# Four attention layers on one core: a copy, additions, gathers, first queries and grouped projections at other places in a hand-written order

## The chip, the cores and the metric

The kernel runs on one core of a Trainium2 chip, on inputs in fp32. The core has TensorE for matmuls (PE in the profile; its weight loads are PEld), VectorE (DVE), ScalarE (ACT), GpSimd (POOL) and SyncE (SP), which issues most DMAs. Matmuls write PSUM, eight banks of 2 KB for each of 128 partitions; TensorE, VectorE and ScalarE use it. The metric is the time of one execution on the device in microseconds (us), as a median over runs.

## The reference

Four residual layers of cross-attention follow each other on `x` of shape (4, 512, 256); the context is (4, 1024, 512). Layers 0, 2 and 3 are alike, "masked", with 16 heads of 64; layer 1 is "grouped", with 16 query heads of 16 that share 4 key and value heads.

```python
# layers 0, 2 and 3 (hidden_states 512 x 256, encoder_hidden_states 1024 x 512, of each of 4 batches)
q, k, v = hidden_states @ Wq, encoder_hidden_states @ Wk, encoder_hidden_states @ Wv
...
logits = jnp.einsum('bhqd,bhkd->bhqk', q, k) * scale + col_bias
out = jnp.einsum('bhqk,bhkd->bhqd', softmax(logits), v)
return out @ Wo + bo + residual
# layer 1
xn = rmsnorm(x, norm_w)
q, k, v = xn @ wq, cond @ wk, cond @ wv
...
attn = softmax(jnp.einsum('bgrtd,bsgd->bgrts', qg, k) * scale)
return residual + jnp.einsum('bgrts,bsgd->btgrd', attn, v) @ wo
```

`col_bias` adds -20 times one minus a mask to the columns of four tokens.

## The kernel before

**Units and steps.** The work is cut into units: one layer, one batch, two masked heads, or a half of a group of grouped heads (`u` from 0 to 7; `h` is `u % 2`). Ninety-six masked and thirty-two grouped units are laid out by `MASKED_TURNS` and `GROUPED_TURNS` into 96 steps, one masked unit `g` each, and in the steps 12 to 19, 22 to 29, 32 to 39 and 68 to 75 a grouped unit `lam` beside it. There is no scheduler: the order in which the last loop calls the helpers is the order of the instructions on each engine.

**A masked unit.** In its step `scores` makes eight tiles of 128 keys by two heads by 512 queries (L854, for the first tile also L860 with the mask), ScalarE copies each to SBUF (L864), and VectorE finds a maximum over them (L871 or L911, then `max_quarters` and `max_everywhere`, L927 to L951). VectorE subtracts it (L959), ScalarE takes exponentials (L965), and POOL sums them (L1004, 7 a unit). In the next step the unit is `g1`: `attend` multiplies with the values (L887), and its sums are turned into reciprocals either on VectorE alone (`normalise`, L911 and L1036 to L1047, then L1073) or with a matmul by ones (`sums_beside`, L1059 and L790 to L792, then L1073). The step after projects two such units together (`project_out`, L1091) and VectorE adds the result to the state (L1113).

**A grouped unit.** In the step before its own it is `coming`: `logits_pair` makes two tiles of logits at a time (L827), which ScalarE copies (L833) and VectorE reduces (`block_max`, L911); there are four such pairs. In its own step POOL subtracts the maximum (L957, 8 a unit), ScalarE takes exponentials, and `attend_grouped` multiplies with the values (L887, 128x32). ScalarE copies one half of the product to SBUF (`keep_even`, L897), VectorE adds the other (`keep_odd`, L901), and after two units (`h` is 1) `turn_grouped` normalises it (L1014 to L1020) and sends it to DRAM or gets the other part from there (L1022, L1025). After four units the grouped projection follows (L1091 and L1113).

**Keys, values, queries.** Keys and values of a pair of masked units are made from the transposed context (`keys`: L540 with the copy L545; `values`: L588, L595). In steps where the third set of buffers is free they are made with seven products in place of eight (`fast_keys`, `fast_values`, L648): POOL first combines weights (L631, four) and, for a batch that is new (`fresh`), the context (L620, four). In `seven_products` the copy L671 of the sixth product into another's bank must be there before that bank and the sixth product's own go on. `project_q` (L751, copy L756) makes the queries of the next masked unit, `follows`. For a first unit of a later layer it stands last but one in the step.

**Loading.** A batch's context rows are gathered by indirect DMAs from POOL (`part_ctx`, L395, each 128 rows), transposed on TensorE at the end of the step (L408, called `rests` in the loop) and kept in DRAM. Steps 1 to 8 do it for batches 1 to 3, two gathers a step up to step 4 and four from step 5.

**The order inside a step.** `fill` is a list of pieces with estimated costs. The loop calls them in turn; `events` (subtractions and exponentials) are let in by estimated time, and `pairs` of a coming grouped unit likewise. A piece's function issues its matmuls and may return a function that issues what follows them on other engines. `late` holds work that runs in `behind_exponentials`, which comes before the first pair of logits, or at the end of the step. `by_ones` is true where a step has both `lam` and `coming`: 28 of the 32.

**PSUM.** `Place` hands out banks: two together, or one. Where both `lam` and `coming` are there (`tabled`), two together come from banks 0 to 3 (scores also 4 and 5) and single ones from 4 to 7. It takes the bank that has been given back the longest in the order of the program (`back`), so what is called later changes which bank the next one gets, and whose last read it waits for:

```python
at = min((n for n in among if n in free), key=lambda n: free[n])
```

Of the kernel before, what the change touches and what calls it, by code (L numbers as in the profile page):

```python
# [80 lines left out]
def kernel(ctx: ExitStack, tc: tile.TileContext, a: dict, out: bass.AP):  # L81
# [740 lines left out]
    def logits_pair(g, i):  # L822
        ws = [Place(), Place()]
        for odd in range(2):
            for j in range(2):
                rows = slice(64 * odd + 32 * j, 64 * odd + 32 * (j + 1))
                nc.tensor.matmul(  # L827
                    ws[odd].ap[:, j * S : (j + 1) * S], lhsT=g.kt[rows, i * P : (i + 1) * P],
                    rhs=g.qt[rows, :], start=True, stop=True,
                )  # L830
        for odd, w in enumerate(ws):
            t = 2 * i + odd
            nc.scalar.copy(g.st[t], w.ap)  # L833
            if tabled[0]:
                w.back()
                block_max(g, t)
            elif t == 0:
                g.mx_place = w
            else:
                w.back()  # L840
                top = g.mx_place.ap
                nc.vector.tensor_tensor(top, top, g.st[t], ALU.max)
# [56 lines left out]
    def keep_odd(g):  # L899
        half = gq[g.b, "o"][64 * g.h : 64 * (g.h + 1), :]  # L900
        nc.vector.tensor_tensor(half, half, g.po[64:128, :], ALU.add)  # L901
        if g.h == 0:
            g.place.back()
# [172 lines left out]
    def project_out(*of):  # L1076

        g = of[0]
        x, acc = xs[g.l, g.b], xs.get((g.l + 1, g.b))
        opens = acc is None  # L1080
        if opens and g.masked:
            acc = new_state(g.l + 1, g.b)
        elif opens:

            acc = xs[g.l + 1, g.b] = x
            x_at[g.l + 1, g.b] = x_at[g.l, g.b]
        w = Place()
        m = w.ap
        for k in range(KC):
            for each in of:  # L1090
                nc.tensor.matmul(  # L1091
                    m[:, k * S : (k + 1) * S], lhsT=each.wo[:, k * P : (k + 1) * P], rhs=each.ot,
                    start=each is g, stop=each is of[-1],
                )
        y = m.rearrange("p (k q) -> p k q", q=S)

        def add_last(q):
            nc.vector.tensor_tensor(acc[:, :, q], y[:, :, q], acc[:, :, q], ALU.add)

        def add():  # L1100
            if g is masked[-1]:
                for i in range(0, NI, 2):
                    add_last(slice(i * P, (i + 2) * P))
                    store(g.b, range(i, i + 2))
                left[g.b] = -1
            elif opens and g.masked:
                bo = columns[f"L{g.l}_xattn_bo"]
                for k in range(KC):
                    nc.vector.scalar_tensor_tensor(
                        acc[:, k, :], y[:, k, :], bo[:, k : k + 1], x[:, k, :], ALU.add, ALU.add  # L1110
                    )
            else:
                nc.vector.tensor_tensor(acc, y, x if opens else acc, ALU.add)  # L1113
            w.back()

        left[g.b] -= len(of)
        return add
# [50 lines left out]
    parts = {}  # L1168
# [19 lines left out]
    rests = [p() for p in parts[-1]]  # L1188
    g0, g1 = masked[0:2]
# [23 lines left out]
    def values(of):  # L1213
        if of.masked:
            return [(1.8, lambda n=n, h=h: v_pair(of, n, h)) for n in range(NI) for h in range(2)]
        return [(1.4, lambda n=n: v_quarter(of, n)) for n in range(4)]

    def idle_set(n):
        if n < 10:
            return 0 < n  # L1220
        return n < len(steps) - 2 and not (
            at(n)[1] or at(n + 1)[1] or at(n + 2)[1] and at(n + 2)[1].first
        )
# [9 lines left out]
    for n in range(len(steps) + 2):  # L1233
# [4 lines left out]
        g1, attended = attended, g  # L1238
        ending = n >= len(steps) - 2

        rests = [p() for p in parts.get(n, ())] if n >= 0 else []
        kk = []
        if g:
            kk = masked[1:2] if n == 0 else masked[g.n + 1 : g.n + 3] if g.n % 2 else []
# [31 lines left out]
        if fast_k or fast_v:  # L1276
            assert 2 in sets_free, n
            combine_weights(kk[0].w["k2"] if fast_k else g.w["v2"])
            fresh = combined_of != (kk[0] if fast_k else g).b
            if fresh:  # L1280
                combined_of = (kk[0] if fast_k else g).b
                combine_context(combined_of)
        else:
            combined_of = None
        if soon and soon.first:
            fetch_whole(soon.b)

# [9 lines left out]
        ready = []  # L1297
        events = []
        late = []
        pairs = []  # L1300

        def pass_events(us):
# [8 lines left out]
        def pair(i):  # L1311
            if i == 0:
                behind_exponentials()
                take_set(coming)
            logits_pair(coming, i)
            if i == NT // 2 - 1:
                max_quarters(coming)
                max_everywhere(coming)
# [44 lines left out]
        if coming:  # L1363
# [3 lines left out]

        fill, of_grouped = (  # L1370
            [
                (1.8 * len(each), lambda each=each: project_out(*each))
                for each in outs if each[0].masked == m
            ]
            for m in (True, False)
        )
        outs = []
        of_queries = []
        if follows and not (follows.l and follows.u == 0):
            of_queries.append((1.7, lambda: project_q(follows)))  # L1380
        if coming and coming.first:
            of_queries += [(1.7, lambda i=i: grouped_q(coming, i)) for i in range(2)]
        if fast_k:
            of_keys = fast_keys(*kk)
            if fresh:
                of_keys[1:4] = of_keys[3:4] + of_keys[1:3]
            fill = of_keys[:2] + fill + of_keys[2:4] + of_queries + of_keys[4:]
        elif fast_v:
            of_values = fast_values(g)
            if fresh:  # L1390
                of_values[1:4] = of_values[3:4] + of_values[1:3]
            fill = of_values[:2] + fill + of_queries + of_values[2:]
        else:
            fill += of_queries
            if kk:
                fill += keys(*kk)
# [3 lines left out]
        if lam:  # L1400

            def attend_grouped():
                while any(of is lam for _, of, _ in events):
                    events.pop(0)[2]()
                lam.v = head(lam).v
                place_out(lam)
                attend(lam)
                give_set(lam)
                late.append(lambda: keep_odd(lam))
                if lam.h == 1:  # L1410
                    late.append(lambda: turn_grouped(lam))
                return lambda: keep_even(lam)

            total, where = 0.0, 0
            while where < len(fill) and total < (8.0 if by_ones and of_values else 9.5):
                total += fill[where][0]
                where += 1
            fill.insert(where, (3.6, attend_grouped))
            if by_ones:
                fill.insert(where, (1.0, lambda: late.insert(0, sums_beside(g1))))  # L1420
        if soon and soon.first:

            def square():
# [8 lines left out]
        if coming and coming.first:  # L1432
            fill += values(coming)
            fill.append((0.0, lambda: drop_whole(coming.b)))
        if follows and follows.l and follows.u == 0:

            fill[-1:-1] = [(1.7, lambda: project_q(follows))]
        if g1 and g and ending:
# [56 lines left out]
```

## Time and profile before

| | |
|---|---|
| median of 3 runs | 3468.09 us (3467.56 to 3470.66) |
| profiled execution | 3467.95 us, span of its instructions 3465.9 |
| mean granted clock of TensorE | 0.999 |
| L1004 on POOL | 668 x 2369 ns |
| L965 on ACT | 1024 x 1058 ns |
| L959 on DVE | 768 x 1212 ns |
| L957 on POOL | 256 x 2381 ns |
| L864 on ACT | 768 x 1047 ns |

The table's lower part is from the profile's list of costliest groups: how often, and how long one is. A group is a line with an engine and a shape; each row also tells how long the engine was idle just before such instructions and what ended most of that. TensorE's matmuls are pipelined, so the duration of one is longer than the distance of two: the distance of two L540 passes on the timeline is 0.43 us, of two L648 of 128 columns 0.11. One fp32 matmul stands there as two passes. The lengths of some steps, from the first scores matmul to the next step's:

| step | us | step | us |
|---|---|---|---|
| 6 | 30.47 | 8 | 32.85 |
| 11 | 49.86 | 31 | 50.17 |
| 12, 22, 68 | 41.54, 41.55, 41.54 | 32 | 42.60 |
| 14, 74 | 40.08, 40.08 | 18, 24, 28, 34, 70 | 40.63, 40.66, 40.63, 40.63, 40.64 |
| 15, 25, 33, 35, 69 | 44.31, 44.31, 44.29, 44.33, 44.33 | 17, 27, 37 | 43.46 each |
| 23, 71 | 44.31, 44.31 | 16, 26, 36, 72 | 41.90, 41.88, 41.91, 41.86 |
| 43, 45 | 31.66, 31.77 | 41, 47, 63, 77 | 34.59, 33.17, 33.18, 37.33 |
| 42, 44 | 28.72, 28.72 | 40, 76 | 32.05, 32.04 |

### The profile page before, as it was taken

How to read it: one execution, taken by the hardware profiler on the slowest of the kernel's cores; microseconds unless marked ns; L12 is line 12 of the kernel's file. 1: busy time of each engine (PE TensorE's matmuls, PEld its weight loads, DVE VectorE, ACT ScalarE, POOL GpSimd, SP SyncE). 2: the span in 40 equal slices, each digit the busy share in tenths (PEclk: the TensorE clock that was granted, in tenths of full speed). 3: DMA queues.
4: the chain of work that ended last, by engine and by line, in shares of the span. 5: the costliest groups of instructions: out<-in, count | busy, mean ns of one | idle time of the engine just before them, and what ended most of it. 6: DMA issues, size and time to landing. Idle time of an engine off the chain costs nothing.

```text
span 3465.9 us, 42986 instructions
## 1 busy us (share of the span) xinstructions
PE 3425.5 (99%) x15634; PEld 1672.4 (48%) x15634; DVE 2970.5 (86%) x3911; ACT 2347.2 (68%) x2727; POOL 2588.8 (75%) x1331
## 2 busy tenths in 40 slices
PE   8999999999999999999999999999999999999998
PEld 4554544445444444444445454554544444454553
DVE  7888788987889878997888888888789987888887
ACT  4676577775877667876566666666677875666664
POOL 5888588884888758888678768677588888769774
PEclk9999999999999999999999999999999999999999
DMA  3232201111100120001001101011101101011100
GB/s 105 64 99 83 78 19 53 34 50 39 54 27 30 46 63 30 26 30 46 27 28 52 40 29 42 28 52 54 39 30 51 36 20 52 28 42 57 30 31 9
DMA packets 146199, 151.71 MB, mean 44 GB/s; under 512 B 23608, under 2 KB 123448, under 8 KB 145476
## 3 DMA queue, kind: packets, MB, share of 16 engines
q1 hardware_dynamic: 142894, 140.05, 12.9%
q0 software_dynamic: 2560, 8.39, 0.8%
q8 instruction: 124, 2.03, 0.2%
q14 instruction: 87, 0.71, 0.1%
q10 hardware_dynamic: 534, 0.52, 0.0%
HBM read 132.15 MB, written 15.73 MB: 43 GB/s over the span
## 4 chain that ended last, share of the span: by engine, by line
PE 90%; DVE 5%; POOL 2%; ACT 2%; issue 1%; DMA 0%; DVEq 0%; ACTq 0%; POOLq 0%
PE ps L887 21%; PE ps L648 18%; PE ps L854 17%; PE ps L588 9%; PE ps L540 8%; PE ps L751 5%; PE ps L827 5%; PE ps L1091 4%; DVE ps L871 1%; POOL st L957 1%; DVE st L959 1%; PE ps L1059 1%; PE ps L728 1%; ACT st L864 1%; PE ps L860 1%
## 5 line engine op out<-in xcount | busy, mean ns | idle before, releaser
L1004 POOL TENSOR_TENSOR st<-st 128x1024 f32<-128x1024 f32 x668 | 1582.5, 2369 | 579.0 <-ACT st L965 534.1
L965 ACT ACTIVATE st<-st 128x1024 f32<-128x1024 f32 x1024 | 1038.9, 1058 | 260.9 <-DVE st L959 136.3
L959 DVE TENSOR_TENSOR st<-st,ps 128x1024 f32<-128x1024 f32 x768 | 883.6, 1212 | 3.3
L887 PE MATMUL ps<-st,v 128*64 128x512 f32 (+1 forms) x4064 | 789.8, 595 | 1.5 <-ACT kt L545 1.5
L957 POOL TENSOR_TENSOR st<-st 128x1024 f32<-128x1024 f32 x256 | 598.1, 2381 | 256.5 <-DVE st L951 256.5
L871 DVE TENSOR_TENSOR ps<-ps,st 128x1024 f32<-128x1024 f32 x476 | 586.7, 1233 | 218.1 <-ACT st L864 174.9
L864 ACT COPY st<-ps 128x1024 f32<-128x1024 f32 x768 | 714.7, 1047 | 79.2 <-PE ps L860 63.9
L854 PE MATMUL ps<-qt,kt 64*128 64x512 f32 x3072 | 712.2, 598 | 6.0 <-DVE every L938 2.6
L911 DVE TRANSPOSE_TENSOR_REDUCE tops<-st 128x32 f32<-128x1024 f32 x448 | 517.1, 1211 | 41.9 <-ACT st L833 41.0
L887 PEld LDWEIGHTS ps<-st,v 128*64 128x64 f32 (+1 forms) x4064 | 239.8, 130 | 536.5 <-issue 447.2
L854 PEld LDWEIGHTS ps<-qt,kt 64*128 64x128 f32 x3072 | 291.5, 186 | 363.4 <-ACT st L864 139.1
L588 PE MATMUL ps<-wv,ctx 128*128 128x256 f32 x1408 | 325.6, 384 | 0.0
L648 PE MATMUL ps<-st 128*128 128x128 f32 (+1 forms) x1572 | 303.3, 341 | 9.9 <-ACT ps L671 7.8
L540 PE MATMUL ps<-ctx,wk 128*128 128x512 f32 x672 | 309.8, 604 | 2.2 <-ACT ctx L420 2.2
L833 ACT COPY st<-ps 128x1024 f32<-128x1024 f32 x256 | 246.7, 1016 | 91.8 <-PE ps L827 91.6
L588 PEld LDWEIGHTS ps<-wv,ctx 128*128 128x128 f32 x1408 | 262.2, 190 | 93.6 <-issue 55.2
L648 PEld LDWEIGHTS ps<-st 128*128 128x128 f32 x1572 | 208.5, 191 | 102.1 <-issue 91.6
L663 ACT COPY st<-ps 128x512 f32<-128x512 f32 x44 | 25.8, 586 | 332.1 <-PE ps L648 332.1
L540 PEld LDWEIGHTS ps<-ctx,wk 128*128 128x128 f32 x672 | 123.4, 191 | 180.0 <-issue 163.4
L751 PE MATMUL ps<-x,wq 128*128 128x512 f32 x384 | 186.3, 608 | 1.3 <-ACT x L383 1.1
L1091 PE MATMUL ps<-ot,wo 128*128 128x512 f32 x384 | 175.2, 598 | 0.7 <-DVE ot L1073 0.7
L827 PE MATMUL ps<-qt,kt 32*128 32x512 f32 x1024 | 171.7, 640 | 1.3 <-ACT st L833 0.7
(190 smaller groups left out, 2980.4 us busy)
## 6 DMA issues: line engine op xcount, KB each, us to landing
ctx<-kept SPq DMA_DIRECT2D x24, 1024.0 KB, 8.1
wk<-in_L_xattn_Wk_dram SPq DMA_DIRECT2D x47, 512.0 KB, 3.6
wv<-in_L_xattn_Wv_dram SPq DMA_DIRECT2D x47, 512.0 KB, 3.6
wq<-in_L_xattn_Wq_dram SPq DMA_DIRECT2D x96, 128.0 KB, 3.6
wo<-in_L_xattn_Wo_dram SPq DMA_DIRECT2D x96, 128.0 KB, 3.7
st<-kept SPq DMA_DIRECT2D x4, 2048.0 KB
qt<-q SPq DMA_DIRECT2D x64, 128.0 KB, 3.7
kept<-st SPq DMA_DIRECT2D x12, 512.0 KB, 3.2
```

What stands on the lines that cost most here:

```text
L540: nc.tensor.matmul(m, lhsT=g.w["k"][:, k, :], rhs=ctx_half[g.b, n][:, k, :], start=(k == 0), stop=(k == KT - 1),)
L588: nc.tensor.matmul(m[:, half * 2 * P : (half + 1) * 2 * P], lhsT=ctx_half[g.b, t // 4][:, k, t % 4 * P : (t % 4 + 1) * P], rhs=g.w["v2"][: ...
L648: nc.tensor.matmul(m if is_keys else m[:, q], lhsT=right[:, k, :] if is_keys else left_[:, k, q], rhs=left_[:, k, :] if is_keys else right ...
L854: nc.tensor.matmul(m[:, j * S : (j + 1) * S], lhsT=g.kt[g.rows[j], keys], rhs=g.qt[g.rows[j], :], start=True, stop=t > 0,)
L864: nc.scalar.copy(g.st[t], m)
L871: nc.vector.tensor_tensor(top, top, g.st[t], ALU.max)
L887: nc.tensor.matmul(g.po[at, :], lhsT=g.v[:, t, rows], rhs=g.st[t][:, j * S : (j + 1) * S], start=(t == first), stop=(t == last),)
L911: nc.vector.tensor_reduce(out_, of.rearrange("p (b x) -> p b x", x=32), AX.X, op, apply_transpose=True)
L957: nc.gpsimd.tensor_tensor(g.st[t], g.st[t], g.mb, ALU.subtract)
L959: nc.vector.tensor_tensor(g.st[t], g.st[t], g.mb, ALU.subtract)
L965: nc.scalar.activation(st, st, AF.Exp)
L1004: nc.gpsimd.tensor_tensor(g.acc, g.st[0] if t == 1 else g.acc, g.st[t], ALU.add)
```

## The change

- In steps that are `by_ones`, `keep_even` (ScalarE's copy of a grouped half) and `keep_odd` with `turn_grouped` no longer run right after the grouped product and in `late`. They go into a new list, `behind_pair`, which is emptied in `pair` right after the next `logits_pair`, thus after the copies of the first pair. In other steps `keep_odd` and `turn_grouped` stay in `late`, as one function.
- In odd steps that are `by_ones`, the addition behind a `project_out` goes into `late` (a new helper, `behind`), thus behind all subtractions of the unit. The turned sums of `sums_beside` are appended to `late` and no longer put at its head.
- `rests`, whose calls issue the gathers and the load of `x`, is made after the combinations of weights and context and not at the head of the step.
- `project_q` for a first unit of a layer stands last but one only where the state it reads is finished late (a new helper, `comes_late`); elsewhere it stands where it does for all other units.
- Where values are made with seven products, for a new batch, the projection of grouped units (`of_grouped`) comes behind the second product and `project_q` behind the fourth; both stood further back or between others. Where the batch is not new, the list `fill`, which is then empty, is left out.

```diff
+    def comes_late(g, n):
+        if g.l == 0 or g.u:
+            return False
+        return step_of[g.l - 1, g.b, 7] >= (n - 1 if g.l == 2 else n - 2)
...
-        rests = [p() for p in parts.get(n, ())] if n >= 0 else []
...
             combined_of = None
+        rests = [p() for p in parts.get(n, ())]
         if soon and soon.first:
             fetch_whole(soon.b)
...
             logits_pair(coming, i)
+            while behind_pair:
+                behind_pair.pop(0)()
             if i == NT // 2 - 1:
...
+        def behind(add):
+            if not by_ones or n % 2 == 0:
+                return add
+            late.append(add)
+
         fill, of_grouped = (
             [
-                (1.8 * len(each), lambda each=each: project_out(*each))
+                (1.8 * len(each), lambda each=each: behind(project_out(*each)))
...
-        if follows and not (follows.l and follows.u == 0):
+        if follows and not comes_late(follows, n):
             of_queries.append((1.7, lambda: project_q(follows)))
...
             if fresh:
                 of_values[1:4] = of_values[3:4] + of_values[1:3]
-            fill = of_values[:2] + fill + of_queries + of_values[2:]
+                fill = of_values[:2] + fill + of_grouped + of_values[2:4] + of_queries + of_values[4:]
+                of_grouped = []
+            else:
+                fill = of_values[:2] + of_queries + of_values[2:]
...
                 give_set(lam)
-                late.append(lambda: keep_odd(lam))
+                if not by_ones:
+                    late.append(keep_others)
+                    return lambda: keep_even(lam)
+                behind_pair.extend([lambda: keep_even(lam), keep_others])
+
+            def keep_others():
+                keep_odd(lam)
                 if lam.h == 1:
-                    late.append(lambda: turn_grouped(lam))
-                return lambda: keep_even(lam)
+                    turn_grouped(lam)
...
             if by_ones:
-                fill.insert(where, (1.0, lambda: late.insert(0, sums_beside(g1))))
+                fill.insert(where, (1.0, lambda: late.append(sums_beside(g1))))
...
-        if follows and follows.l and follows.u == 0:
+        if follows and comes_late(follows, n):

             fill[-1:-1] = [(1.7, lambda: project_q(follows))]
```

1 line of the change is left out of this document (added).

## The prediction

> **What bounds it now.** A step here is one masked unit; step n begins at its first scores matmul (the L854 just ahead of L860 on the timeline), so the length of a step is the distance of two such starts. I read the page first, then TensorE's own waits, then the timelines of a few steps.
>
> ```profile
> PE 3425.5 (99%) x15634; PEld 1672.4 (48%) x15634; DVE 2970.5 (86%) x3911; ACT 2347.2 (68%) x2727; POOL 2588.8 (75%) x1331
> PE 90%; DVE 5%; POOL 2%; ACT 2%; issue 1%; DMA 0%; DVEq 0%; ACTq 0%; POOLq 0%
> ```
>
> TensorE sets the end, and the change adds and removes no matmul: it can only open or close gaps on TensorE. The gaps are small, so the whole stake is some tens of us. TensorE's waits, as "waiting tile and line, releaser: total us, times, longest":
>
> ```profile
> PE ps L648 <- ACT ps L671: 7.8, 7, 1.4
> PE ps L648 <- POOL st L631: 2.1, 1, 2.1
> PE ps L887 <- ACT kt L545: 1.5, 2, 0.7
> ```
>
> The first two are gaps that the change aims at; the third is one that it makes more frequent. The timeline of step 13 (from 475.3), a step with a grouped half, shows TensorE, then ScalarE, then VectorE (start, us, line, shapes, count):
>
> ```profile
> 500.06 1.08 PE L1059 MATMUL ps<-st,ones 128*64 128x512 f32 x4
> 501.06 3.64 PE L887 MATMUL ps<-st,v 128*32 128x512 f32 x32
> 504.64 1.14 PE L827 MATMUL ps<-qt,kt 32*128 32x512 f32 x8
> 505.71 1.98 PE L540 MATMUL ps<-ctx,wk 128*128 128x512 f32 x4
> 507.79 2.04 PE L827 MATMUL ps<-qt,kt 32*128 32x512 f32 x8
> ...
> 502.68 0.57 ACT L545 COPY kt<-ps 128x512 f32<-128x512 f32 x1
> 503.15 2.95 ACT L965 ACTIVATE st<-st 128x1024 f32<-128x1024 f32 x3
> 506.12 0.58 ACT L897 COPY o<-ps 64x512 f32<-64x512 f32 x1
> 506.72 1.93 ACT L833 COPY st<-ps 128x1024 f32<-128x1024 f32 x2
> ...
> 495.79 1.22 DVE L1113 TENSOR_TENSOR x<-ps,x 128x1024 f32<-128x1024 f32 x1
> 509.88 6.87 DVE L911 TRANSPOSE_TENSOR_REDUCE tops<-st 128x32 f32<-128x1024 f32 x6
> 516.93 2.37 DVE L911 TRANSPOSE_TENSOR_REDUCE tops<-st 128x32 f32<-128x1024 f32 x2 [0.19 <-ACT st L833]
> ```
>
> The second pair of logits (L827 at 507.79) lasts 2.04 instead of 1.14: it waits for the copies of the first pair (L833), which stand behind the copy of the grouped half (L897). Last, the head of step 77:
>
> ```profile
> 2866.02 1.23 DVE L1113 TENSOR_TENSOR x<-ps,x 128x1024 f32<-128x1024 f32 x1 [5.72 <-PE ps L1091]
> 2869.87 1.12 PE L854 MATMUL ps<-qt,kt 64*128 64x512 f32 x2 [0.59 <-DVE short L1041]
> 2871.63 2.83 PE L854 MATMUL ps<-qt,kt 64*128 64x512 f32 x6 [0.64 <-DVE ot L1073]
> ```
>
> VectorE idled 5.72 us for the grouped projection (L1091), the last matmul of step 76, and the normalisation behind it (L911 to L1073) then kept PSUM banks that the next scores wanted.
>
> **The edits that gain.**
> - *Gathers behind the weight combinations.* In step 8 four gathers (L395, 0.95 us each, 1.25 apart) stand on POOL before L631, and L648 idles 2.12 us for it. Step 6, the same work, lasts 30.47 us, step 8 32.85: 2.4 gained. The gathers come 2.9 us later (four L631), 12.3 where four L620 go before (steps 1 and 7); landing 3.2 to 5.4 us after issue, the last of step 7 lands by about 281.7, its transposes begin at 281.87. That cover is nearly used up: a loss of up to 1 there. On SP only the load of x moves, behind three weight loads of some 0.4 us each; it is read at the end of its step.
> - *First queries earlier.* In steps 47, 63 and 77 project_q moves between the sixth and the seventh product, where TensorE idled 1.27, 1.27 and 0.8 us for L671: its 1.72 us fill the gap. Steps 47 and 63 last 33.17 and step 45 without the gap 31.77: 1.4 each, 0.9 in step 77. In step 31 the wait for qt (0.69) and the late maximum in step 32 (0.68) go: steps 11 and 12, where the query already stands early, last 49.86 and 41.54 against 50.17 and 42.60: 1.4.
> - *Grouped projection earlier in steps 40 and 76.* VectorE no longer idles; normalisation ends before the next step's third tile of scores. Step 41 falls from 34.59 to step 43's 31.66: 2.9. Step 77 (37.33) falls to 31.77, 5.56 in all, of which 4.6 is this. In steps 40 and 76 themselves the 1.37 us wait for L671 shrinks, but the addition L1113 (1.22) now stands between subtractions and delays the exponentials ahead of L671: 0.7 of 1.5 gained each; bounds 0 and 1.5.
>
> Sum: 2.4+2.8+0.9+1.4+2.9+4.6+1.4 = 16.4 us.
>
> **The edits that cost.** Sixteen odd steps carry a grouped half; twelve of them (13, 15, 17, 23 and so on) keep both additions and sums in `late`.
> - *Additions behind subtractions.* The addition now runs after eight L959 instead of after three; VectorE's sum is unchanged and the sums' transpose (L790 at 502.57) starts when it did. The earlier subtractions bring nothing: ScalarE works without a gap from 496.50, and before that it waited for POOL's L957, not for VectorE. But the two banks of the projection are given back later too, so in the built order the ones-matmul L1059 takes the query's bank, and the grouped half's output (L887) takes the bank of the first key copy, L545. L887, due at 501.06, must wait for 503.25: 2.2 us. It is the wait that steps 23 and 71 have already (0.73). By each step's own rows L545 ends 2.2 late in 13, 15, 25, 33, 35 and 69 and 0.5 late in 17, 27, 37 and 73, where POOL starts 1.7 us earlier; 23 and 71 go to 2.2, since their query's copy (0.57) and one exponential more now stand before L545. In the first six, ScalarE is then idle when the first pair comes: the second pair's wait falls from 0.9 to 0.2 and a 0.16 wait ahead of the first goes. Net 2.2-0.7-0.1 = 1.4 each, 8.4; four times 0.5, 2.0; twice 1.4, 2.8: 13.2 us lost.
> - *Copy behind the first pair's.* What is queued behind L897 changes places only; L901 and the normalisation L1014 to L1020 (3.15 us on VectorE in odd steps) now come after two L911 instead of before eight. With the pairs 1.4 later I count the last L911 at 46.2 us of a step of 45.7, where it ended 0.27 before the step's end: 0.8 later against TensorE. So POOL's L957 of the next step starts 0.8 late, and so do its exponentials: step 18 against step 14 shows the slope (L957 begins at 3.02 and 2.17, exponentials end at 29.12 and 28.29). Even steps: 12, 22, 32 and 68 follow no such step and gain 0.5 each (0.58 of copy, less overlap); ten lose 0.8-0.5 = 0.3; 14 and 74 had slack. Net +1.0; bounds -7.7 (0.57 gained in ten, no slip) and +3. The store of the normalised half and its four reloads (L1022, L1025, SP) leave some 4 us later; their reader is a projection more than 15 us on.
> - *The clock.* New gaps of 2.2 us come eight times. The windows view gives busy us of each engine and the granted clock (PEclk) for three stretches:
>
> ```profile
> 2868.36:2871.78 3.42, 2.19 (x8) 0.54 (x7) 3.14 (x12) 1.71 (x2) 3.34 (x3) 1.00 0.99 370
> 2871.78:2875.19 3.41, 3.41 (x10) 1.39 (x12) 2.61 (x3) 1.32 (x2) 3.33 (x5) 0.50 0.05 20
> 298.13:301.54 3.41, 1.93 (x16) 1.74 (x16) 3.18 (x7) 0.59 (x1) 2.78 (x4) 1.00 0.71 181
> ```
>
> After two gaps of 0.6 us the clock was 0.50 for 3.41 us, which costs 1.7; after the gap of 2.12 in step 8 it stayed full, and after six of 1.3 to 1.5 too. So eight gaps cost between 0 and 8x1.7 = 13.6. Nearest is step 8, one long gap, which cost nothing; but the head of step 77 shows that less can do, so I take two of eight: 3.4.
>
> [...]
>
> **Sum.** -16.4+13.2+1.0+3.4 = +1.2 on the profiled execution's 3467.95 (span 3465.9 and 2.05 around it), which lies 0.14 under the median of 3468.09: about 3469.
>
> **Rivals.**
> 1. *The new bank costs nothing* (faster). If L545 came before the sums were done, the eight long and four short waits go (-13.2), the six odd steps keep 0.86 and steps 23 and 71 0.8 (-6.8), and without slip the even steps gain 7.7: 3468-16.4-6.8-7.7 = 3437. For it: eight subtractions in a row end 1.1 us sooner for the later tiles. Against it: ScalarE has no gap there to close. It decides once the long waits are under 1.2 us, 8 us below the forecast.
> 2. *The clock* (slower). Six or more half-clock windows instead of two: seven would be 3469+5x1.7 = 3478. For it: the gap is longer than those that set it off. Against it: step 8. It decides from six windows, 3476.
> 3. *The gains at 41 and 77 don't come* (slower). If the next step's banks still stand behind L1041 and L1073, 2.9+4.6+1.4 go, and with an early gather's landing lost (1) the time is 3479. Against it: VectorE would be done 3 us before the third tile.
>
> That the edits leave the order as it was is excluded: the built order differs in ten steps on TensorE and in all grouped steps on VectorE and ScalarE.
>
> **How the numbers follow.** A measurement of this kernel tells 0.2% (6.9 us: under 3461.1, over 3475.0) from no change. Forecast 0.50 (0.42 within that, 0.06 below, 0.02 above), rival 1 0.18, rival 2 0.18, rival 3 0.14 (0.02 of it within). Faster 0.24, same 0.44, slower 0.32. Range: low -16.4+13.2-7.7 = -10.9, 3457; high with 16.4 cut to 14.9 and seven or eight windows, +13, 3481. The forecast alone: 3461 to 3475. Some 0.13 below and 0.07 above are left out.
>
> **What would show it.** L887 with 2.2 us idle before it, released by L545, in eight steps; L827's second pair back to 1.35; no idle at L648 in steps 8, 47 and 63; no wait on L1041 or L1073 at the head of 41 and 77; odd grouped steps near 45.7 us, even ones near 41; PEclk rows at 0.50 after some of the long gaps. Wrong if L887 doesn't wait, or if the pairs' copies, not the bank, still decide the odd steps.

## The result, and the profile after

| | median us | lowest to highest | runs |
|---|---|---|---|
| before | 3468.07 | 3467.43 to 3470.66 | 16 |
| changed | 3475.62 | 3469.40 to 3482.55 | 16 |

The ratio is 1.0021, 95% interval [1.0014, 1.0028]. That is 7.5 us more, inside the range of 3457 to 3481 and 6.6 above the forecast of 3469; by the forecast's own bound for no change, 3475.0, it is just slower. The more telling number is the spread: 3.2 us before, 13.2 after. The profiled execution of the changed kernel is one of its long ones, 3482.06 us (span 3480.3).

TensorE's own work has not changed, and it still sets the end. The page, its busy times and its chain of what ended last:

```profile
PE 3430.2 (99%) x15634; PEld 1673.7 (48%) x15634; DVE 2968.1 (85%) x3911; ACT 2346.4 (67%) x2727; POOL 2587.2 (74%) x1331
PE 84%; POOL 6%; DVE 6%; ACT 4%; issue 1%; DMA 0%; DVEq 0%; ACTq 0%; POOLq 0%
```

The chain now runs 84% on TensorE instead of 90: POOL's share is 6% instead of 2, ScalarE's 4 instead of 2. TensorE's waits, as "waiting tile and line, releaser: total us, times, longest":

```profile
PE ps L887 <- ACT kt L545: 19.0, 12, 2.2
...
PE ps L648 <- ACT ps L671: 3.2, 4, 1.3
...
PE ps L827 <- ACT st L833: 1.1, 6, 0.2
```

The two gaps that the change aimed at are mostly gone: L648 waits 3.2 us for L671 instead of 7.8, and its 2.1 for POOL's L631 is no longer in the list. The wait of L887 for the first key's copy has grown from 1.5 us in two steps to 19.0 in twelve. The timeline of step 13 (from 473.60), TensorE, then ScalarE, then VectorE:

```profile
498.39 1.08 PE L1059 MATMUL ps<-st,ones 128*64 128x512 f32 x4
501.64 5.34 PE L887 MATMUL ps<-st,v 128*32 128x512 f32 x32 [2.17 <-ACT kt L545]
506.91 1.14 PE L827 MATMUL ps<-qt,kt 32*128 32x512 f32 x8
507.98 1.98 PE L540 MATMUL ps<-ctx,wk 128*128 128x512 f32 x4
509.90 1.35 PE L827 MATMUL ps<-qt,kt 32*128 32x512 f32 x8
...
501.02 0.57 ACT L545 COPY kt<-ps 128x512 f32<-128x512 f32 x1
501.49 2.95 ACT L965 ACTIVATE st<-st 128x1024 f32<-128x1024 f32 x3
508.14 1.93 ACT L833 COPY st<-ps 128x1024 f32<-128x1024 f32 x2 [3.70 <-PE ps L827]
...
499.77 1.22 DVE L1113 TENSOR_TENSOR x<-ps,x 128x1024 f32<-128x1024 f32 x1
500.90 0.70 DVE L790 STREAM_TRANSPOSE ot<-ps 128x512 f32<-128x512 f32 x1
```

L887 waits 2.17 us for L545, which stands in ScalarE's queue behind exponentials until 501.02. The second pair (L827 at 509.90) is back to 1.35 us. And the 32 passes of L887, whose duration was 3.64 us before, take 5.34: the clock granted was 0.50 from 502.00 to 505.42. The windows view (busy us of each engine, then PEclk, the granted clock) shows it for three stretches:

```profile
495.18:498.59 3.41, 3.41 (x10) 1.34 (x10) 3.41 (x4) 3.41 (x5) 3.41 (x2) 1.00 0.00 0
498.59:502.00 3.41, 1.24 (x8) 0.16 (x8) 3.34 (x6) 3.41 (x5) 3.26 (x2) 1.00 0.00 0
502.00:505.42 3.42, 3.42 (x20) 0.87 (x16) 1.33 (x2) 2.44 (x3) 3.34 (x2) 0.50 0.02 5
```

TensorE was busy 1.24 us of the middle stretch; the next stretch was granted 0.50. In this execution the same happens after all eight long waits, with TensorE busy 1.24 to 1.27 us of the stretch before.

### The profile page after: what moved, and what is told of

It is laid out like the page before. It is cut to its first block, busy times and chain, and to the rows that moved or that the text cites. A ratio compares the mean times of both kernels' runs of the same rounds, so it can differ in the third digit from the quotient of the medians.

```text
span 3480.3 us, 43017 instructions
## 1 busy us (share of the span) xinstructions
PE 3430.2 (99%) x15634; PEld 1673.7 (48%) x15634; DVE 2968.1 (85%) x3911; ACT 2346.4 (67%) x2727; POOL 2587.2 (74%) x1331
## 4 chain that ended last, share of the span: by engine, by line
PE 84%; POOL 6%; DVE 6%; ACT 4%; issue 1%; DMA 0%; DVEq 0%; ACTq 0%; POOLq 0%
PE ps L887 19%; PE ps L648 18%; PE ps L854 16%; PE ps L588 8%; PE ps L540 7%; POOL st L957 6%; PE ps L827 5%; PE ps L751 4%; PE ps L1091 4%; ACT st L965 2%; DVE ps L871 1%; DVE tops L911 1%; DVE st L959 1%; ACT st L833 1%; PE ps L728 1%
## 5 line engine op out<-in xcount | busy, mean ns | idle before, releaser
L887 PE MATMUL ps<-st,v 128*64 128x512 f32 (+1 forms) x4064 | 803.3, 610 | 19.0 <-ACT kt L545 19.0
L957 POOL TENSOR_TENSOR st<-st 128x1024 f32<-128x1024 f32 x256 | 597.8, 2377 | 284.3 <-DVE st L951 284.3
L854 PE MATMUL ps<-qt,kt 64*128 64x512 f32 x3072 | 705.1, 596 | 5.0 <-DVE every L938 4.9
L887 PEld LDWEIGHTS ps<-st,v 128*64 128x64 f32 (+1 forms) x4064 | 242.6, 132 | 565.4 <-issue 461.2
L854 PEld LDWEIGHTS ps<-qt,kt 64*128 64x128 f32 x3072 | 289.6, 186 | 354.9 <-ACT st L864 139.8
L648 PE MATMUL ps<-st 128*128 128x128 f32 (+1 forms) x1572 | 303.0, 341 | 3.2 <-ACT ps L671 3.2
L648 PEld LDWEIGHTS ps<-st 128*128 128x128 f32 x1572 | 208.7, 191 | 95.6 <-issue 87.9
L663 ACT COPY st<-ps 128x512 f32<-128x512 f32 x44 | 25.8, 586 | 331.8 <-PE ps L648 331.8
L827 PE MATMUL ps<-qt,kt 32*128 32x512 f32 x1024 | 168.4, 640 | 1.1 <-ACT st L833 1.1
## 6 DMA issues: line engine op xcount, KB each, us to landing
wk<-in_L_xattn_Wk_dram SPq DMA_DIRECT2D x47, 512.0 KB, 3.6
wv<-in_L_xattn_Wv_dram SPq DMA_DIRECT2D x47, 512.0 KB, 3.5
kept<-st SPq DMA_DIRECT2D x12, 512.0 KB, 3.2
```

The lines of the kernel that those rows point to most:

```text
L648: nc.tensor.matmul(m if is_keys else m[:, q], lhsT=right[:, k, :] if is_keys else left_[:, k, q], rhs=left_[:, k, :] if is_keys else right ...
L854: nc.tensor.matmul(m[:, j * S : (j + 1) * S], lhsT=g.kt[g.rows[j], keys], rhs=g.qt[g.rows[j], :], start=True, stop=t > 0,)
L887: nc.tensor.matmul(g.po[at, :], lhsT=g.v[:, t, rows], rhs=g.st[t][:, j * S : (j + 1) * S], start=(t == first), stop=(t == last),)
L957: nc.gpsimd.tensor_tensor(g.st[t], g.st[t], g.mb, ALU.subtract)
```

## The experiments

The tables below give lengths of steps from one profiled execution of each kernel; where a step holds a stretch of 3.41 us at a granted clock of 0.50, that is marked with h. It makes the step about 1.7 us longer: step 15 took 47.37 us with one (changed) and 45.68 without (sums made twice, below).

### The parts by themselves

Four kernels take the change apart. Additions in their old place (against the changed kernel):

```diff
         def behind(add):
-            if not by_ones or n % 2 == 0:
-                return add
-            late.append(add)
+            return add
```

> The changed kernel with one part undone: the additions stand where they stood before, so the grouped half's output takes the query's bank again; the copy behind the first pair and the three moves stay. Theory (the wait for the first key's copy L545 plus the half-clock windows that it sets off are the whole loss): the 2.2 us waits before L887 go in eight steps and 0.5 us waits in four, 3469.4 - 8 x 2.2 - 4 x 0.5 = about 3450 us, no granted clock of 0.50 in the grouped steps, and run times within 3 us of each other. Rival (the moved copy with its later normalisation is what costs): the odd steps stay over 47 us and the time over 3465. Rival (the wait alone, the clock not bound to it): about 3450 too, but with windows of 0.50 still in the grouped steps and run times scattered over 10 us.

Only the additions late (against the kernel before):

```diff
+        def behind(add):
+            if not by_ones or n % 2 == 0:
+                return add
+            late.append(add)
...
-                (1.8 * len(each), lambda each=each: project_out(*each))
+                (1.8 * len(each), lambda each=each: behind(project_out(*each)))
...
-                fill.insert(where, (1.0, lambda: late.insert(0, sums_beside(g1))))
+                fill.insert(where, (1.0, lambda: late.insert(1 if late else 0, sums_beside(g1))))
```

> The kernel before with only the additions put behind the subtractions in the twelve grouped odd steps; nothing else is moved. Theory: L887 waits 2.2 us for L545 in steps 13, 15, 25, 33, 35, 69, and less where the next query is not yet projected early; without the copy's move the second pair still waits somewhat less: 6 x 1.4 to 2.2 + 4 x 0.5 + up to 2 x 1.4 = 10 to 18 us, and 0 to 8 half-clock windows of 1.7 us: 3480 to 3490, scattered. Rival (the new bank costs nothing): 3468 within 2 us, no wait at L887 beyond the 0.7 of two steps. Rival (the wait without the clock): 3478 to 3486 with run times within 3 us of each other.

Only the copy moved (against the kernel before):

```diff
-                late.append(lambda: keep_odd(lam))
-                if lam.h == 1:
-                    late.append(lambda: turn_grouped(lam))
-                return lambda: keep_even(lam)
+                if not by_ones:
+                    late.append(keep_others)
+                    return lambda: keep_even(lam)
+                behind_pair.extend([lambda: keep_even(lam), keep_others])
```

(with `keep_others` and the emptying of `behind_pair` as in the change.)

> The kernel before with only the copy of the grouped half put behind the first pair's copies. Theory: the second pair no longer waits 0.9 us (odd steps 0.6 to 0.9 shorter), even steps 12, 22, 32, 68 are 0.47 shorter, ten other even steps 0.4 longer because normalisation and the last maxima end later: about 3468 - 10 - 2 + 4 = 3460, at most 3468. Rival (the slip of the maxima decides): the even steps after grouped odd steps are over 0.8 longer and the time is over 3472.

Only the three other moves (against the changed kernel, `behind` as in the first of these):

```diff
-                if not by_ones:
-                    late.append(keep_others)
-                    return lambda: keep_even(lam)
-                behind_pair.extend([lambda: keep_even(lam), keep_others])
+                late.append(keep_others)
+                return lambda: keep_even(lam)
...
-                fill.insert(where, (1.0, lambda: late.append(sums_beside(g1))))
+                fill.insert(where, (1.0, lambda: late.insert(0, sums_beside(g1))))
```

> The kernel before with only the three other moves: gathers later, first queries earlier, last grouped projections earlier. Copy and additions are where they were before. Theory: the moves' gains are what the step lengths of the changed kernel show (2.4 in step 8, 2.8 in 41, 5.7 in 77, 1.3 and 1.5 in 47 and 63, 0.4 each in 40 and 76, 1.4 about 31 and 32): 3468 - 16 = 3452 us, steps 13 to 39 and 66 to 75 as before but for 23 and 71. Rival (the gains depend on the late additions or the later copy): less than half of them, over 3460.

| | additions in place | additions late alone | copy alone | three moves alone |
|---|---|---|---|---|
| median us | 3448.78 | 3483.71 | 3466.42 | 3452.66 |
| lowest to highest | 3448.17 to 3449.16 | 3480.19 to 3483.99 | 3463.0 to 3469.64 | 3451.94 to 3453.08 |
| ratio to before | 0.9943 [0.9929, 0.9957] | 1.0042 [1.0028, 1.0055] | 0.9991 [0.9982, 1.0] | 0.9954 [0.9941, 0.9968] |

| step | before | changed | additions in place | additions late alone | copy alone | three moves alone |
|---|---|---|---|---|---|---|
| 8 | 32.85 | 30.46 | 30.47 | 32.82 | 34.47 h | 30.47 |
| 15 | 44.31 | 47.37 h | 43.59 | 45.69 | 43.57 | 44.30 |
| 17 | 43.46 | 43.94 | 43.46 | 43.97 | 43.45 | 43.46 |
| 18 | 40.63 | 41.02 | 41.05 | 40.63 | 41.06 | 40.62 |
| 22 | 41.55 | 41.07 | 41.09 | 41.56 | 41.08 | 41.52 |
| 25 | 44.31 | 47.39 h | 43.57 | 47.39 h | 43.57 | 44.30 |
| 41 | 34.59 | 31.83 | 31.83 | 36.13 h | 36.28 h | 31.83 |
| 77 | 37.33 h | 31.66 | 31.66 | 37.33 h | 37.24 h | 31.93 |

The three moves alone give 15.7 us (from 3468.34, measured beside them, to 3452.66). The copy gives 3.9 more (3452.66 to 3448.78). The additions are the loss, with or without the rest, but not by the same amount: alone they cost 15.4 us (within the 3480 to 3490 expected), on top of the other parts 26.8. By the steps without half-clock stretches it is 10.4 against 18.9. The difference of 8.5 has two halves: where the additions alone are late, the late product also ends the wait of the second pair (0.7 in six steps), which is gone already where the copy is moved; and without the earlier query steps 23 and 71 keep their old wait of 0.73 instead of 2.16. Rivals that blamed the copy, or that tied the moves' gains to it, fall: with the additions in place and everything else as changed, no grouped step holds a half-clock stretch (mean granted clock 0.999) and the runs lie within 1.0 us of each other. The expectation for the copy alone was too hopeful: by steps it brings 2.5 us, not 8, and by its median 1.9, since only six odd steps gain, 0.74 each, and steps 23 and 71 gain nothing without the earlier query; its runs scatter over 6.6 us.

### The clock

The changed kernel with TensorE work in the gap: the ones-matmul made twice, and three times, in the eight steps with the long wait.

```diff
-        for j in range(2):
+        for j in list(range(2)) * times:
...
-                fill.insert(where, (1.0, lambda: late.append(sums_beside(g1))))
+                fill.insert(where, (1.0, lambda: late.append(sums_beside(g1, 2 if n in LONG else 1))))
```

> The changed kernel with the ones-matmul L1059 made twice (same operands, same bank) in the eight steps with the long wait: 1.0 us of TensorE work in the gap of 2.17, whose end stays. In five of the traces so far ten stretches of 3.41 us on the clock's own grid with matmuls busy under 0.40 were followed by a stretch at 0.50, those from 0.45 up mostly not. Theory (a gap halves the clock if it lies wholly in one stretch of the grid): with at least 0.66 busy no stretch is halved; the eight steps are 45.7 us in every run and the time 3469.4 within 1.5 us. Rival (the wait for ScalarE, however filled, or the copy's place sets it off): as the changed kernel, 3469 to 3483 scattered, median about 3475. Rival (the extra work adds its own time): 3469.4 + 8 x 1.0 = 3477 without scatter.

> The same with the ones-matmul made three times: 2.0 us of work, the gap nearly closed. Theory: the end of the wait is set by L545, so nothing is added and nothing saved against sums made twice: 3469.4 within 1.5 us, no clock of 0.50 in the grouped steps. Rival (idleness itself costs beyond the wait's end, at the restart): 8 x 0.2 to 0.5 less than with sums made twice. Rival (the work adds its own time): 3469.4 + 16 = 3485.

Measured: 3467.42 us (3467.07 to 3468.34, 11 runs) and 3467.56 (3467.15 to 3468.51, 11 runs); ratio to before 0.9998 [0.9989, 1.0007] and 0.9999 [0.999, 1.0008]. More work, and 8 us less than the changed kernel. Step 15 takes 45.68 and 45.71 us where it took 47.37. Both times lie 2 us below what was expected, 3469.4 within 1.5: that had taken the fastest run of the changed kernel for one without half clock, but by these times it still holds about one stretch. The windows view at step 15 with the sums made twice:

```profile
585.09:588.50 3.41, 2.11 (x17) 0.42 (x16) 3.31 (x6) 3.41 (x5) 3.31 (x2) 1.00 0.00 0
588.50:591.91 3.41, 3.41 (x33) 0.92 (x25) 0.42 (x1) 1.48 (x2) 3.33 (x2) 1.00 0.02 5
```

A stretch with 2.11 us busy is followed by full clock, where the changed kernel's, with 1.24 to 1.27, were followed by 0.50; the mean granted clock of the profiled run is 1.000 here, made twice or three times. So the wait for ScalarE alone did not bring half clock here: with TensorE busy in it, the clock stayed full. And the end of the wait does not move with what fills it: made twice or three times, the time is the same. What the wait itself costs, against the kernel with additions in place, stands here without the clock: 3467.42 - 3448.78 = 18.6 us, which is 2.1 in eight steps and 0.5 in four.

The kernel with the additions late alone has the same 2.2 us gap, and only one of its six was followed by half clock. The windows view of that kernel, at step 13 and at step 25:

```profile
499.19:502.60 3.41, 1.79 (x6) 0.20 (x4) 3.41 (x4) 3.41 (x5) 3.33 (x2) 1.00 0.00 0
502.60:506.02 3.42, 2.87 (x28) 0.94 (x32) 2.17 (x4) 3.35 (x5) 3.26 (x3) 1.00 0.02 5
1011.20:1014.60 3.40, 1.23 (x8) 0.16 (x8) 3.33 (x6) 3.40 (x5) 3.26 (x2) 1.00 0.00 0
1014.60:1018.00 3.40, 3.40 (x20) 0.87 (x16) 1.35 (x2) 2.45 (x3) 3.31 (x2) 0.50 0.00 0
```

Both gaps are 2.17 us long. The one at step 13 is cut by a border between stretches of 3.41 us, so that no stretch is emptier than 1.79 busy, and the next is granted 1.00; the one at step 25 lies inside a stretch, 1.23 is busy, and the next is granted 0.50. Both belong to one grid: from the border at 502.60 to that at 1014.60 it is 512.0 us, 150 stretches of 3.413, and the half-clock records of the changed kernel are whole numbers of 3.413 us apart too.

### The bank, or the late addition

The changed kernel, late additions and all, with the product ahead of the ones-matmul in the odd grouped steps, so that the two swap banks:

```diff
-            fill.insert(where, (3.6, attend_grouped))
-            if by_ones:
-                fill.insert(where, (1.0, lambda: late.append(sums_beside(g1))))
+            if by_ones and n % 2:
+                fill.insert(where, (4.6, lambda: (attend_grouped(), late.append(sums_beside(g1)))[:0]))
+            else:
+                fill.insert(where, (3.6, attend_grouped))
+                if by_ones:
+                    fill.insert(where, (1.0, lambda: late.append(sums_beside(g1))))
```

> The changed kernel, late additions and all, with one swap in the odd grouped steps: the grouped half's product L887 is issued ahead of the ones-matmul L1059, so L887 takes the query's bank and L1059 the bank of the first key's copy L545. Theory (it is the bank and not the late addition that costs): L887 starts when due, L1059 is due 3.6 us later than L887 was and finds L545 done, no wait over 0.3, no halved clock: 3467.5 (the changed kernel without halved clock, as with the sums made twice) - 8 x 2.17 - 4 x 0.5 = about 3448 us within 2 us. Rival (the late addition delays VectorE, whichever bank is taken: the sums' transposes come 1.5 to 2 us later and the maxima with them): 3452 to 3460. Rival (the product is not ready at that date and waits for its last exponential): a new wait of 0.5 to 1.5 us at L887 for L965, 3452 to 3460.

Measured: 3451.7 us (3450.85 to 3452.15), ratio 0.9952 [0.9939, 0.9966]. Step 13 of that kernel, TensorE, then VectorE:

```profile
497.17 3.64 PE L887 MATMUL ps<-st,v 128*32 128x512 f32 x32
500.74 1.08 PE L1059 MATMUL ps<-st,ones 128*64 128x512 f32 x4
501.75 1.14 PE L827 MATMUL ps<-qt,kt 32*128 32x512 f32 x8
...
498.55 1.21 DVE L1113 TENSOR_TENSOR x<-ps,x 128x1024 f32<-128x1024 f32 x1
501.93 0.72 DVE L790 STREAM_TRANSPOSE ot<-ps 128x512 f32<-128x512 f32 x1 [2.17 <-PE ps L1059]
```

L1113 is as late as in the changed kernel, and L887 starts without a gap: the odd steps are those of the kernel with additions in place (43.57 in step 15), and no stretch is halved in the grouped steps (mean granted clock 0.999). So 15.7 of the 18.6 us hang on which matmul gets the bank, with the additions as late as before. That the ones-matmul now has L545's bank follows from the order of the calls; a trace does not name banks. The swap is not quite free: VectorE now waits 2.17 us for the sums, and twelve even steps are 0.15 to 0.3 longer than with the additions in place, 2.9 us in the two medians. The time misses the first theory's 3448 within 2 and ends just under the second's 3452 to 3460: the first has the odd steps right, the second what is left in the even ones. The wait for a last exponential that the third feared did not come.

The other way to take the wait away is to issue the product when the copy is done: one key projection later, and the first pair with it.

```diff
-            while where < len(fill) and total < (8.0 if by_ones and of_values else 9.5):
+            while where < len(fill) and total < (8.0 if by_ones and of_values else 11.2 if n in LATER else 9.5):
...
-            pairs += [((18.0 if coming.first else 12.0) + 2.5 * i, i) for i in range(NT // 2)]
+            pairs += [((18.0 if coming.first else 13.7 if n in LATER else 12.0) + 2.5 * i, i) for i in range(NT // 2)]
```

> The changed kernel, with the grouped half's product (and the first pair) one key projection later in the eight steps whose wait is 2.2 us; everything else as changed. Theory (the price is the date of L545's end, 501.6, against the date at which L887 is due): L887 is due 1.98 us later and waits at most 0.4, the eight steps fall from 45.7 to about 43.8, no clock of 0.50 there, 3469.4 - 8 x 1.9 = about 3454 us within 2 us from run to run. Rival (the late addition costs whichever bank is taken: the next key projections then wait for their own copies): the eight steps stay over 45 us, 3465 or more.

Measured: 3477.62 us (3473.53 to 3479.69), ratio 1.0026 [1.0015, 1.0037]. The wait shrank to 0.45 us and step 15 to 43.97, as expected; but step 16 grew from 42.28 (sums made twice) to 43.98, and so in every step behind one of the eight, three of them with half clock on top (mean granted clock 0.998). The two timelines tell why. First this kernel at step 13:

```profile
500.29 3.64 PE L887 MATMUL ps<-st,v 128*32 128x512 f32 x32 [0.45 <-ACT kt L545]
503.86 1.14 PE L827 MATMUL ps<-qt,kt 32*128 32x512 f32 x8
...
548.90 2.04 PE L827 MATMUL ps<-qt,kt 32*128 32x512 f32 x8 [1.04 <-ACT st L833]
...
521.96 18.69 POOL L957 TENSOR_TENSOR st<-st 128x1024 f32<-128x1024 f32 x8 [9.15 <-DVE st L951]
```

Then the kernel with the sums made twice, whose wait ends at 500.45:

```profile
500.45 3.64 PE L887 MATMUL ps<-st,v 128*32 128x512 f32 x32 [1.29 <-ACT kt L545]
504.02 1.14 PE L827 MATMUL ps<-qt,kt 32*128 32x512 f32 x8
...
522.12 18.70 POOL L957 TENSOR_TENSOR st<-st 128x1024 f32<-128x1024 f32 x8 [9.12 <-DVE st L951]
```

With the product later the first pair (L827) starts at nearly the same date, so the maxima end and POOL's L957 starts at nearly the same date (521.96 against 522.12). TensorE reached step 14 at 517.10 instead of 518.98, and step 14 took 41.89 instead of 40.17: its second pair (548.90) waits for the copies of the first, which come no sooner. Filling a gap with work pulled forward saved nothing here, where the loop through the pair, its copies, the maxima, POOL's subtractions and the exponentials was not shortened: the wait at L887 costs as much as it does because it delays the first pair, not because TensorE stands still. Neither theory had this: the rival's time (over 3465) came, but not the long odd steps by which it was to come.

### The copy's slip, and a better kernel

Additions in place, and the copy behind the first pair in even grouped steps and step 13 only:

```diff
-                if not by_ones:
+                if not by_ones or n % 2 and n != 13:
```

> The kernel with additions in place (3448.8 us) and the copy behind the first pair only in the even grouped steps and in step 13; in the other odd grouped steps copy and normalisation stand where they were before. Theory (normalisation among the maxima of an odd step ends the maxima 0.9 us later, and the next even step pays it): steps 16, 18, 24, 26, 28, 34, 36, 38, 70, 72 fall by 0.87 to what 12, 22, 68 have (41.1) or 0.47 under before, steps 15, 23, 25, 33, 35, 69, 71 rise by 0.74: 3448.8 - 8.7 + 5.2 = 3445.3 us. Rival (the slip comes from the even steps' own copy): the even steps stay, 3448.8 + 5.2 = 3454 us.

The three moves alone, and the copy on VectorE, ahead of L901:

```diff
-    def keep_even(g):
+    def keep_even(g, on=None):
...
-        nc.scalar.copy(gq[g.b, "o"][64 * g.h : 64 * (g.h + 1), :], g.po[0:64, :])
+        (on or nc.scalar.copy)(gq[g.b, "o"][64 * g.h : 64 * (g.h + 1), :], g.po[0:64, :])
...
+                if by_ones:
+                    late.append(lambda: keep_even(lam, nc.vector.tensor_copy))
                 late.append(keep_others)
-                return lambda: keep_even(lam)
+                return None if by_ones else lambda: keep_even(lam)
```

> The kernel with the three moves alone (3452.7 us), and the copy L897 of the grouped half on VectorE in place of ScalarE, after the sums' normalisation and just ahead of L901; additions in their old place. VectorE idles 1.7 us there in odd steps, and ScalarE is the engine that the first pair's copies wait on. Theory (the copy costs as 0.58 us of ScalarE ahead of the first pair, and the slip comes from normalisation behind the first maxima): odd steps fall by 0.74 to 43.6 and the even ones by 0.47, without the 0.9 slip: 3445.65 - 7 x 0.74 = about 3440.5 us. Rival (VectorE has no room: 0.6 us more there ends the maxima later and the next step pays it): even steps 0.4 to 0.6 longer in ten places, 3446 or more.

| step | three moves alone | additions in place | copy in even steps and 13 | copy on VectorE |
|---|---|---|---|---|
| 15 | 44.30 | 43.59 | 44.31 | 43.56 |
| 16 | 41.90 | 42.31 | 41.80 | 41.80 |
| 18 | 40.62 | 41.05 | 40.15 | 40.18 |
| 22 | 41.52 | 41.09 | 41.06 | 41.07 |
| median us | 3452.66 | 3448.78 | 3445.65 | 3442.36 |

The first is 3443.86 to 3446.97, ratio 0.9934 [0.9921, 0.9948], where 3445.3 was expected. The slip is thus made in the odd step and paid in the next even one: 0.9 us in step 18, but only 0.5 in 16, 26, 36 and 72, for a reason that stays open. This kernel moves copy and normalisation together; that normalisation is what counts is read from VectorE at step 13 with the additions in place, which has no idle time from the first maxima to the last:

```profile
505.04 2.37 DVE L911 TRANSPOSE_TENSOR_REDUCE tops<-st 128x32 f32<-128x1024 f32 x2 [1.99 <-ACT st L833]
507.44 0.69 DVE L901 TENSOR_TENSOR o<-o,ps 64x512 f32<-64x512 f32 x1
...
510.59 6.87 DVE L911 TRANSPOSE_TENSOR_REDUCE tops<-st 128x32 f32<-128x1024 f32 x6
517.49 0.61 DVE L927 TENSOR_REDUCE ps<-tops 128x32 f32<-128x256 f32 x1
```

With the copy on VectorE both gains come together: 3442.36 us (3441.9 to 3442.89), ratio 0.9925 [0.9912, 0.9939], 2 us short of the expectation; 1.3 of them are in steps 47, 61, 76 and 93, each 0.2 to 0.4 longer than with the three moves alone, for a reason that stays open. It beats both kernels, by 25.8 us the one before. VectorE at step 13 of that kernel:

```profile
502.06 0.69 DVE L1073 TENSOR_TENSOR ot<-ps,ot 128x512 f32<-128x512 f32 x1
502.78 0.69 DVE L897 COPY o<-ps 64x512 f32<-64x512 f32 x1
503.50 0.69 DVE L901 TENSOR_TENSOR o<-o,ps 64x512 f32<-64x512 f32 x1
...
506.64 6.87 DVE L911 TRANSPOSE_TENSOR_REDUCE tops<-st 128x32 f32<-128x1024 f32 x6
513.91 2.37 DVE L911 TRANSPOSE_TENSOR_REDUCE tops<-st 128x32 f32<-128x1024 f32 x2 [0.40 <-ACT st L833]
```

The copy and the whole normalisation fit into the time in which VectorE used to idle, and the last maxima wait for their copies again, not for VectorE.

## Why the forecast held, and what was off

- **Gathers, first queries, grouped projections.** Forecast 16.4 us, measured 15.7 by the three moves alone. Step by step in the changed kernel: step 8 fell by 2.39 (2.4), 41 by 2.77 (2.9), 77 by 5.67 (5.56 in all, the two terms on it together), 47 and 63 by 1.29 and 1.52 (1.4 each); 31 and 32, by the three moves alone, by 1.37 (1.4). Steps 40 and 76 fell by 0.43 each instead of 0.7: the wait for L671 went from 1.37 to 0.75 us, not further. The feared late landing of a gather does not show: step 7, whose last gather now starts at 278.74 us, takes 33.41 in both kernels.
- **The bank.** This was read off the built order, and everything about it came: which copy L887 waits for, some 2.16 us in the eight steps, 0.5 in four. Less the relief at the second pair, the eight steps are 1.4 us longer without the clock (45.68 against 44.31 in step 15). All twelve together are 13.0 us longer (13.2).
- **The copy.** Four even steps gained 0.46 (0.5), ten lost 0.4 (0.3), steps 14 and 74 lost 0.1 each (nothing). The cause was right; the sum is 2.4 us lost (1.0), within its bounds.
- **The clock.** This is the term that was mis-sized. The forecast took two half-clock stretches of eight, 3.4 us. The profiled execution has all eight. Without any, the kernel takes 3467.5 (the sums made twice or thrice), so the median of 3475.62 holds (3475.62 - 3467.5)/1.69 = 4.8 of them, with 1.69 the difference of step 15 between the two. That is 8.1 us against 3.4, and 4.7 of the 6.6 that the forecast was short. The 4.8 is good to about one: the profiled execution, with eight by its trace, comes out as 8.6 by the same division, since its first step begins 1.2 us later. The remaining 1.9 are 0.7 from the moves and 1.4 from the copy, less 0.2 from the bank.

The step that failed in it was the row it leaned on: "after the gap of 2.12 in step 8 it stayed full". That was one position of the gap on the grid: it lasted from 300.06 to 302.18 us, and a stretch ended at 301.54, within it. (The six other gaps that the forecast gives as 1.3 to 1.5 us are 1.23 to 1.37 on the trace; nothing rests on it.) In the run with the copy alone the same gap was followed by half clock, as the windows view at step 8 shows:

```profile
299.64:303.05 3.41, 1.29 (x12) 1.10 (x11) 3.27 (x4) 1.23 (x2) 2.70 (x5) 1.00 0.73 204
303.05:306.46 3.41, 3.41 (x16) 3.41 (x17) 3.41 (x4) 0.41 (x1) 2.06 (x3) 0.50 0.28 84
```

How many should have been taken can be worked out from the traces. A gap of 2.16 us lies wholly in a stretch of 3.41 for (3.41 - 2.16)/3.41 = 0.37 of all positions, which makes 3 of 8 if every gap fell anywhere on the grid with equal chance. It does not, because a half-clock stretch delays all that comes behind it. From the gap of step 13 to that of 15 it is 86.7 us without a half-clock stretch, 25.4 stretches of the grid, and 88.4 with one, 25.9. So a gap that hits leaves the next nearly where it stood, and that one hits too. Following the seven distances between the eight gaps of the trace over all starting positions gives 4.0 to 4.2 hits on average if the gap must lie wholly inside, and 4.8 to 5.0 if 0.1 us of it may stand out. This is an estimate from the gaps of this one trace, and it takes for granted that the place on the grid decides, as the two gaps of 2.17 us with the additions late alone suggest; the mean of the 16 runs, 3475.8, gives 4.9 by the division above.

- **The rivals.** Rival 1 (the bank costs nothing) did not come: ScalarE had no gap to close, as was said against it, and L545 starts 27.42 us into step 13 in both kernels. Rival 2 (six and more half-clock stretches, from 3476) is what the times of seven of the sixteen runs tell, from 3477.8 up, the profiled one with its eight among them; three of them lie over the range. The median ends between the forecast's own 3475 and this rival's 3476. Rival 3 (no gains at 41 and 77) did not come.

## What to carry to other kernels

Moving an instruction behind others on one engine also moves the date at which its buffer comes free, and with a rotating set of banks it can change which bank a later matmul gets: read from the built order what the new bank waits for, before counting what the move saves. Apart from the clock, the gap on TensorE cost here what it delayed, so ask which later work starts earlier if a gap closes; closing it with work pulled forward gave back nothing. And where a change makes the runs scatter, a gap that sometimes costs nothing is not free: its price is its chance, over all runs, and one profile shows only one draw.

## What the hardware showed unexpectedly

In the trace of the changed kernel the granted clock is 1.00 in mid-kernel but for eight records of 0.50, each 3.413 us long, with 1.00 again behind each. They start at 502.00, 590.75, 932.08, 1020.83, 1362.16, 1450.91, 2580.72 and 2669.47 us: 26, 100, 26, 100, 26, 331 and 26 times 3.413 us apart. The one mid-kernel record of 0.50 in the kernel before, at 2871.78 us, is 3.413 us long as well. Counted from the start of each span, it lies 0.92 us off the grid of those eight.

How long TensorE was busy in a stretch, and what clock the next was granted:

- The eight of the changed kernel that hold its long waits were busy 1.24 to 1.27 of 3.41 us, step 25 with the additions late alone 1.23 and step 8 with the copy alone 1.29: the next was granted 0.50 in all ten.
- Three others, idle 1.30 to 1.62 us of theirs, were busy 1.79 (step 13, additions late alone), 1.93 (step 8, before) and 2.11 us (step 15, sums made twice): the next was granted 1.00.
- With scores matmuls alone (64x512, 64 partitions of input) busy time does not tell the two apart. In the kernel before, 2.19 us busy with eight passes (at 2868.36, the head of step 77) was followed by 0.50, but 2.18 with twelve (at 2796.68) by 1.00, and so were the four of the changed kernel with 2.19 us busy and twelve to fourteen passes of L854 and L860 (at 737.52, 1167.60, 1597.68 and 2816.24).

What sets the one at 2868.36 apart, the number of passes or something else, stays open.
